# Two graph-attention layers: the second pair's projection goes through DRAM, residual loads are spread, the opening gets four row buffers

## The chip, the cores and the metric

The kernel runs on one core of one Trainium2 chip. A core has five engines, each with its own queue that it works off in order: TensorE (PE in the profile; its weight loads are a row of their own, PEld), VectorE (DVE), ScalarE (ACT), GpSimd (POOL) and SyncE (SP), which here only starts DMAs. Engines wait for one another by semaphores. DMAs are started by SP, ACT and POOL.

The metric is device time in microseconds (us). Before the change the median of three runs was 2545.72 us (2536.66 to 2552.91). The profile comes from one more execution, which took 2237.41 us.

## The reference

Two graph-attention layers run on N = 4096 nodes with a dense 0/1 adjacency matrix of int32 that holds about 32 neighbours per row (each entry is set with a chance of 1/256, the matrix is made symmetric). Cut to what matters:

```
def gat0(x, adj):                       # 8 heads of 128
    Wh  = einsum('nf,hfd->hnd', x, W)
    e   = leaky_relu(Wh@a1 [:,:,None] + Wh@a2 [:,None,:], 0.2)
    att = softmax(where(adj > 0, e, -9e15))
    hp  = elu(att @ Wh)                 # heads side by side, 1024 wide
    return hp @ W_out + b_out
x = layernorm(x + gat0(x, adj))
def gat1(x, adj):                       # 4 heads of 64
    xt  = einsum('ni,hio->hno', x, W)
    e   = leaky_relu(src + dst, 0.2)
    att = softmax(where(adj > 0, e, -inf))
    return att @ xt                     # heads side by side, 256 wide
x = layernorm(x + gat1(x, adj))
```

## The kernel before, in words

**Layer 1 (gat0) is sparse.** The factors exp of the scores let the attention be a product and a maximum, without an exponential per edge. A table in DRAM holds for each node its 256 features of x, a one, the two score factors of each head, and words of adjacency bits. There are two copies of the table, used by the phases in turn. The rows are handled in 32 tiles of 128 and in 8 phases of four tiles. A tile takes 8 steps of 16 target rows, so the loop has NG = 256 steps n (from L1209 on). For a step, GpSimd starts four indirect DMAs (L882), each of which gathers 128 rows of the table by a list of ids into a row buffer G (pool "rows", six buffers; gathers run AHEAD = 5 steps before their use). Every fourth step there is one shared gather more (Gs, L897). VectorE weighs the gathered rows (L987 to L1002), TensorE adds them up in PSUM (po, L1010), ScalarE divides (ag, L1034), TensorE and ScalarE transpose (pa L1041, aT L1044). Per tile, `close0` does the heads' projection (ph L1070), elu, the output projection (py L1093), the residual, the normalisation, stores the row tile in x1_d (L1118) and transposes it into x1T (pz L1121, L1122). Its pieces are worked off one per step from a list named `late`. When eight tiles, a chunk, are done, the following tiles' pieces are given the scores of layer 2 for that chunk and two steps of the projection for layer 2 (`step1`, pw L858 and wh L867: 16 matmuls, then 8 activations, for four row tiles).

**The lists of ids** of phase s + 2 are made while phase s runs: `words_of` loads adjacency (aq, L572), turns it to bf16 (mb, L582 or L584) and counts it into words by TensorE (L596); `lists_of` takes the largest entries by eights on VectorE (L673), transposes (lst L733, pl L738) and writes ids (L751).

**The opening** makes the lists of phase 0 out of adjacency loaded into the row buffers (tiles Ga), and the scores of layer 1: `Scores.chunk` for each of four chunks, with factors L418 (VectorE), L422 and L425 (ScalarE) in a tile `row` with one buffer, a transpose (pr L433), a store of the row to r_d by ScalarE's queue (L443), and the factors of the table's rows (L454, L457), stored into the table's tail columns by `publish` (L703). `inputs` copies x into the table (L549). Words of phase 1 begin in the opening (L827): six pieces there, the others two per step in the loop. After the opening come the first gathers.

The whole of layer 1, with the opening, has its order on each engine written out by hand (manual schedule): an instruction stands in its engine's queue where the program text puts it.

**Layer 2 (gat1) is dense.** Two pairs of heads g, four chunks c of 1024 target columns, and 32 source tiles j. For each (g, c, j) SP loads a 128 x 1024 block of the adjacency (L1308, four buffers), ScalarE makes a mask of it (mb, L1309), VectorE makes the weights of two heads (e, L1496), and TensorE multiplies them with the projected features wh (L1327, 16 matmuls) and with the row factors for the denominators (L1339, 8 matmuls). The features of the first pair are projected in layer 1, those of the second pair in (g, c) = (0, 2) by eight steps of `prepare1` from `late`. y_sb holds the residual rows, loaded from x1_d by four DMAs of 1 MB each (L1470). `unit1` divides and adds after each chunk; the last units also normalise (L1424 to L1439), in the end with four scalings in a row on ScalarE (L1436), each followed by a store. Layer 2's order on each engine is set by a scheduler, not by hand.

The last lines of the program run a general path if a flag is set; with this input it isn't.

Of the kernel before, what the change touches and what calls it, by code (L numbers as in the profile page):

```python
# [262 lines left out]
def fast_path(  # L263
# [72 lines left out]
    class Scores:  # L336
# [29 lines left out]
        def chunk(self, k, src):  # L366
# [41 lines left out]
            def factors():  # L408
                if k == 0:
# [5 lines left out]
                row = held["row"] = small.tile(  # L415
                    [P, HC], F32, tag="row", name=f"row_{n}_{k}", bufs=1
                )
# [71 lines left out]
    zero = const.tile([1, RW], F32, name="zero")  # L489
    nc.gpsimd.memset(zero, 0.0)  # L490
# [55 lines left out]
    def inputs(i, k):  # L546
        if k == 0:
            nc.sync.dma_start(table[i][N : N + 1, :], zero)
        nc.sync.dma_start(table[i][ts(k, CH), 0:F], x[ts(k, CH), :])  # L549

    lists = [None] * NPH
    words = {}

    def words_of(s):
# [7 lines left out]
        def load(m):  # L562

            k, t, q = m // (PT * PQ), m // PQ % PT, m % PQ
            if s == 0:
                G = gpool.tile([P, NB, RW], F32, tag="G", name=f"Ga_{m}")
# [20 lines left out]
        def count(m):  # L587
# [17 lines left out]
            if t == PT - 1 and q == PQ - 1:  # L605
# [9 lines left out]
                )  # L615

# [174 lines left out]
    def opening():  # L791
# [51 lines left out]
    def prepare1(g, pool):  # L843

        cj = sc1.cj
        wh = pool.tile([P, NT, 2, D1], F32, tag="wh", name=f"wh_1_{g}", bufs=1)
        w_sb = pool.tile([P, KC, 2 * D1], F32, tag="w", name=f"w_1_{g}", bufs=1)

        def first():
            nc.sync.dma_start(  # L850
                w_sb, w1f[:, ts(g, 2 * D1)].rearrange("(c p) d -> p c d", p=P)
            )

        def step(m):
            pw = ps_m.tile([P, 4, 2 * D1], F32, tag="m", name=f"pw_1_{g}_{m}")
            for jj in range(4):
                for c in range(KC):
# [3 lines left out]
                        w_sb[:, c, :],  # L861
                        start=(c == 0),
                        stop=(c == KC - 1),
                    )
            for jj in range(4):
                for k in range(2):
                    nc.scalar.activation(  # L867
                        wh[:, m + jj, k, :],
                        pw[:, jj, ts(k, D1)],
                        AF.Copy,  # L870
                        scale=cj[:, m + jj, 2 * g + k : 2 * g + k + 1],
                    )

        return wh, first, step
# [174 lines left out]
    def close0(i, aT):  # L1049
# [64 lines left out]
        def flip(k):  # L1114
# [10 lines left out]
            if turned[q] == CT:  # L1125
                fs = sc1.chunk(q, x1T[0])
                steps = [lambda m=m: step1(m) for m in range(q * CT, q * CT + CT, 4)]
# [17 lines left out]
        due = st0["due"] = st0.pop("then", {})  # L1145
        due.setdefault(0, []).append(add)
# [16 lines left out]
    now1, first1, step1 = prepare1(0, wpool)  # L1163
    late.add(load1, first1, lambda: sc1.weights(a1_sb, w1T_sb))
# [7 lines left out]
    FIRST_COUNT = 10  # L1172
# [22 lines left out]
    with tc.manual_schedule():  # L1195
# [12 lines left out]
        shared[0].weigh()  # L1208
        for n in range(NG + SOON + 1):  # L1209
            i, o, s = n // GT, n % GP, n // GP  # L1210
            busy = 0.0
            if n < NG:
# [10 lines left out]
                if o == GP - AHEAD and s + 2 < NPH:  # L1223
# [10 lines left out]
                if n % 4 == 1 and 0 < n // 4 <= NCH:  # L1234
                    inputs(1, n // 4 - 1)
# [113 lines left out]
    def unit1(g, c, po):  # L1349
# [48 lines left out]
        def norm(i0):  # L1398
# [51 lines left out]
    def verdict():  # L1450
# [17 lines left out]
    late.add(  # L1468
        *(
            lambda c=c: nc.sync.dma_start(  # L1470
                y_sb[:, ts(c, CT), :], x1_d[ts(c, CT)].rearrange("t p f -> p t f")
            )
            for c in range(NCH)
        )
    )
    for g in range(G):
        wh = now1
        for c in range(NCH):
            po = open1(g, c)
            if c == NCH - 2 and g + 1 < G:  # L1480
                now1, first1, step1 = prepare1(g + 1, rpool)
                late.add(first1, *(lambda m=m: step1(m) for m in range(0, NT, 4)))
# [3 lines left out]
            for j in range(NT):  # L1486
                if g + c == 0 and j == NT - CT:
                    late.all()
# [12 lines left out]
                if j >= 2:  # L1501
                    late.some(2 if g + c == 0 else 1)
# [81 lines left out]
```

## Time and profile before

| what | value |
|---|---|
| median of three runs | 2545.72 us (2536.66 to 2552.91) |
| profiled execution | 2237.41 us, its span 2235.6 us |
| mean granted TensorE clock, profiled | 0.957 |
| busy: PE, DVE, ACT, POOL | 89%, 87%, 39%, 48% of the span |
| DMA traffic | 443.55 MB, mean 198 GB/s |
| first gather (Gs, L897) | 85.67 us after the start |
| last gather | 1477.9 us |
| first mask weights of layer 2 (e, L1496) | 1511.5 us |
| last scaling (L1436) begins | 2227.8 us |

The span runs from the first to the last instruction of the one core. "Busy" counts instructions' own time; waiting is told apart by what ended it ("<-" and the releaser). "Issue" is idle time in which the engine waited for nothing that the profile shows. A granted clock of 1.00 is TensorE's full speed. A row of waits reads: engine, tile and line that waited, what released it, total us, times, longest us. A row with "q" behind the engine's name (SPq) is the queue of the engine's DMA issues.

### The profile page before, as it was taken

The numbers are of one execution on the slowest core, as the hardware profiler recorded it, in microseconds if no ns is written. First come the engines' busy times: TensorE is split into PE (matmuls) and PEld (weight loads), VectorE is DVE, ScalarE is ACT, GpSimd is POOL, SyncE is SP. The second block draws the span as 40 slices with busy tenths as digits, with TensorE's granted clock in tenths as the row PEclk, the third lists the DMA queues.
The fourth block names the chain that finished last, engine by engine and source line by source line (L and its number), as shares of the span: only waits on it lengthen the run. The fifth ranks groups of instructions, "written<-read, shape, count | busy, mean of one in ns | idle before, by whom it ended". The sixth has DMA issues, their size and how long they took to land.

```text
span 2235.6 us, 35623 instructions
## 1 busy us (share of the span) xinstructions
PE 1996.7 (89%) x12481; PEld 1142.5 (51%) x12481; DVE 1955.2 (87%) x4117; ACT 882.9 (39%) x1826; POOL 1077.9 (48%) x1154
## 2 busy tenths in 40 slices
PE   5487888989989999989888899888999999999996
PEld 2255566666666666666665667664424333333332
DVE  6579899999989999988999988747998899999996
ACT  1333424424334334334432233234445444465563
POOL 1377777777777777777777777730000000000000
PEclk9589999989999999999999999999999999999998
DMA  9799677578567677667665555538665566676762
GB/s 323 192 297 258 180 206 245 152 198 249 158 178 239 180 182 231 192 178 216 205 143 150 150 153 139 147 114 298 218 196 191 168 216 217 204 229 223 224 211 87
DMA packets 184149, 443.55 MB, mean 198 GB/s; under 512 B 60788, under 2 KB 92535, under 8 KB 183959
## 3 DMA queue, kind: packets, MB, share of 16 engines
q1 hardware_dynamic: 125814, 265.99, 37.9%
q0 software_dynamic: 52224, 169.97, 27.8%
q10 hardware_dynamic: 5920, 5.21, 0.8%
q8 instruction: 101, 1.65, 0.3%
q14 instruction: 90, 0.73, 0.1%
HBM read 426.04 MB, written 23.40 MB: 201 GB/s over the span
## 4 chain that ended last, share of the span: by engine, by line
PE 44%; DVE 33%; DMA 11%; issue 4%; POOL 4%; ACT 2%; SPq 1%; DVEq 0%; ACTq 0%; POOLq 0%
PE po L1327 20%; PE po L1339 10%; PE po L1010 9%; DMA G<-table,ids 7%; DVE e L988 5%; DVE e L994 5%; DVE e L1002 5%; POOL G L882 4%; DVE side L987 2%; DVE side L996 2%; PE py L1093 1%; DVE lst L673 1%; PE pw L858 1%; DVE hT L1084 1%; DVE side L916 1%
## 5 line engine op out<-in xcount | busy, mean ns | idle before, releaser
L882 POOL DMA_INDIRECT G<-table,ids x1024 | 977.9, 955 | 319.0 <-issue 234.1
L1496 DVE SCALAR_TENSOR_TENSOR e<-rb,pj,mb 128x1024 f32<-128x1024 f32 x512 | 635.5, 1282 | 58.9 <-PE po L1339 27.8
L1010 PE MATMUL po<-G,e 128*128 128x257 f32 x2048 | 553.5, 416 | 75.9 <-DVE e L1002 75.6
L1327 PE MATMUL po<-e,wh 128*32 128x512 f32 x4096 | 531.3, 595 | 7.1 <-DVE e L1496 7.1
L1010 PEld LDWEIGHTS po<-G,e 128*128 128x128 f32 x2048 | 392.1, 201 | 222.2 <-DVE e L1002 119.8
L1309 ACT ACTIVATE mb<-aq 128x1024 bf16<-128x1024 int32 x256 | 271.1, 1061 | 321.5 <-DVE e L1496 264.4
L1339 PE MATMUL po<-e,cj 128*32 128x512 f32 x2048 | 315.2, 594 | 0.0
L1411 POOL TENSOR_SCALAR nm<-nm 128x4 f32<-128x4 f32 x6 | 5.5, 911 | 640.6 <-ACT ju L1410 640.6
L1327 PEld LDWEIGHTS po<-e,wh 128*32 128x32 f32 x4096 | 149.7, 110 | 290.9 <-issue 252.6
L1034 ACT ACTIVATE ag<-po,rd_all 128x256 f32<-128x256 f32 x256 | 121.5, 475 | 321.0 <-DVE rd_all L1030 317.0
L1044 ACT COPY aT<-pa 128x256 f32<-128x256 f32 x256 | 94.8, 370 | 377.9 <-PE pa L1041 371.1
L1010 PE MATMUL po<-own,eo 128*128 128x257 f32 x512 | 166.3, 407 | 62.5 <-ACT ag L1034 57.8
L988 DVE TENSOR_TENSOR e<-rb,side 128x512 f32<-128x512 f32 x256 | 175.8, 687 | 9.1 <-DVE side L987 0.3
L994 DVE TENSOR_TENSOR e<-e,side 128x512 f32<-128x512 f32 x256 | 175.7, 686 | 8.9
L1002 DVE TENSOR_TENSOR e<-e,side 128x512 f32<-128x512 f32 x256 | 175.7, 686 | 8.8
L1010 PE MATMUL po<-Gs,e_s 32*128 32x257 f32 x512 | 182.0, 435 | 1.5 <-DVE e_s L931 1.5
L1070 PE MATMUL ph<-aT,w_sb 128*128 128x128 f32 x1024 | 145.6, 287 | 11.8 <-DVE hT L1084 11.6
L1339 PEld LDWEIGHTS po<-e,cj 128*32 128x32 f32 x2048 | 80.3, 110 | 147.3 <-issue 135.2
L1070 PEld LDWEIGHTS ph<-aT,w_sb 128*128 128x128 f32 x1024 | 135.1, 199 | 26.4 <-DVE hT L1084 12.4
L584 ACT ACTIVATE mb<-aq,half 128x1024 bf16<-128x1024 int32 x112 | 128.6, 1151 | 36.4 <-issue 18.6
L1093 PE MATMUL py<-wo_sb,hT 128*128 128x256 f32 x512 | 125.4, 388 | 0.0
L1010 PEld LDWEIGHTS po<-Gs,e_s 32*128 32x128 f32 x512 | 76.0, 185 | 89.3 <-issue 87.1
(171 smaller groups left out, 1907.3 us busy)
## 6 DMA issues: line engine op xcount, KB each, us to landing
aq<-in_adjT SPq DMA_DIRECT2D x256, 512.0 KB
aq<-in_adj SPq DMA_DIRECT2D x112, 512.0 KB
rb<-r_d SPq DMA_DIRECT2D x48, 512.0 KB
G<-table,ids POOLq DMA_INDIRECT x1024, 3.4
table<-in_x SPq DMA_DIRECT2D x8, 1024.0 KB
table<-tail SPq DMA_DIRECT2D x56, 98.0 KB
own<-table SPq DMA_DIRECT2D x32, 152.5 KB
Ga<-in_adj SPq DMA_DIRECT2D x8, 512.0 KB
```

Source lines behind the costliest of these rows:

```text
L584: nc.scalar.activation(mb, raw.pop(m), AF.Sign, bias=half[:, 0:1])
L882: nc.gpsimd.indirect_dma_start(out=G[:, b, :], out_offset=None, in_=table[s % 2][:, :], in_offset=bass.IndirectOffsetOnAxis(ap=lists[s][:, ...
L988: nc.vector.tensor_tensor(e, rb[:, :, ts(n % GT, T)].unsqueeze(1).to_broadcast(sh), f_p[:, :, 0:H0].unsqueeze(3).to_broadcast(sh), ALU.mult,)
L994: nc.vector.tensor_tensor(e, e, f_p[:, :, H0:].unsqueeze(3).to_broadcast(sh), ALU.max)
L1002: nc.vector.tensor_tensor(e, e, nb_p.unsqueeze(2).to_broadcast(sh), ALU.mult)
L1010: nc.tensor.matmul(po, w.rearrange("p h t -> p (h t)"), v[:, 0 : F + 1], start=first, **kw)
L1070: nc.tensor.matmul(phs[k][:, hh, :], w_sb[:, c, ts(h, D0)], aT[:, c, h, :], start=(c == 0), stop=(c == KC - 1),)
L1093: nc.tensor.matmul(pys[0], hT[:, h, :], wo_sb[:, h, :], start=False, stop=(h == H0 - 1))
L1309: nc.scalar.activation(mb, aq, AF.Relu, scale=OPEN)
L1327: nc.tensor.matmul(po[q][ts(b, DQ), :], wh[:, j, k, d : d + DQ], es[k][:, ts(q, HB)], start=(j == 0), stop=(j == NT - 1), tile_position=(0 ...
L1339: nc.tensor.matmul(po[NQ][r0 : r0 + DQ, :], sc1.cj[:, j, 2 * g + k : 2 * g + k + 1].to_broadcast([P, DQ]), es[k][:, ts(q, HB)], start=(j = ...
L1496: nc.vector.scalar_tensor_tensor(e, rb[k], sc1.pj[:, j, h : h + 1], mb, ALU.max, ALU.min)
```

## The change

1. **Opening.** The four chunks' `row` tiles of layer 1's scores lie in the four buffers of the weights' tag "e" instead of in one buffer.
2. **Zero rows.** The zero row of both tables is written at the start, from a tile of the pool `two`. The copies of x into the second table stand at steps n = 10, 14, 18, 22 instead of 5, 9, 13, 17.
3. **Words of phase 1.** When the opening's score pieces are used up, the first seven loads (EARLY = 7) are issued together, three into the usual buffers and four into row buffers. Their seven conversions and counts come after the first gathers, just ahead of the loop; the other nine follow two per step, each issuing a further load. The words of phase 2 begin at step 13 instead of 10, and its lists are turned at step 31 instead of 27.
4. **Projection for the second pair.** `prepare1` becomes a class, `Projected`. Six of the eight steps of the second pair, those of chunks 0 to 2, are done in layer 1's loop two tiles after the first pair's; ScalarE writes them into a staging tile (wo, in the one buffer of tag "row") and SP stores them in a DRAM tensor wh1_d, 256 KB each. Layer 2 fetches these 1.5 MB into wh, and only the steps of the last chunk stay there.
5. **Residual loads.** One 1 MB load of y_sb at every eighth step j of the first unit, instead of four in a row from `late`; `late` gives one piece per step everywhere, and is not emptied at j = 24.
6. **Last scaling.** In the last unit the odd ones of the scalings are done by VectorE, the even ones by ScalarE.

The diff, cut to its core:

```diff
@@ Scores.chunk, factors
-                row = held["row"] = small.tile(
-                    [P, HC], F32, tag="row", name=f"row_{n}_{k}", bufs=1
-                )
+                if n == 0:
+                    row = two.tile([P, HC], F32, tag="e", name=f"row_{n}_{k}", bufs=4)
+                else:
+                    row = small.tile([P, HC], F32, tag="row", name=f"row_{n}_{k}", bufs=1)
+                held["row"] = row
...
@@ inputs
-        if k == 0:
-            nc.sync.dma_start(table[i][N : N + 1, :], zero)
+        if i + k == 0:
+            for t in table:
+                nc.sync.dma_start(t[N : N + 1, :], zero[0:1, :])
...
@@ words_of
-            if s == 0:
-                G = gpool.tile([P, NB, RW], F32, tag="G", name=f"Ga_{m}")
+            if s == 0 or (s == 1 and 3 <= m < EARLY):
+                G = gpool.tile([P, NB, RW], F32, tag="G", name=f"Ga_{s}_{m}")
...
+        if s == 1:
+            def then(m):
+                convert(m)
+                count(m)
+                k = m + EARLY if m < 3 else m + 3 if m >= EARLY else NW
+                if k < NW:
+                    load(k)
+            for m in range(EARLY):
+                load(m)
+            return [lambda m=m: then(m) for m in range(NW)]
...
@@ opening
-        firsts.add(*words_of(1))
...
-            if m in (24, 26, 31, 33, 35, 37):
-                firsts.some()
+            if not scored.items and not firsts.items:
+                firsts.add(*words_of(1))
...
@@ prepare1 -> class Projected, step(m, away=False)
+            if away:
+                o = small.tile([P, 4 * 2 * D1], F32, tag="row", name=f"wo_1_{g}_{m}", bufs=1)
             for jj in range(4):
                 for k in range(2):
+                    a = 2 * jj + k
                     nc.scalar.activation(
-                        wh[:, m + jj, k, :],
+                        o[:, ts(a, D1)] if away else self.wh[:, m + jj, k, :],
...
+            if away:
+                nc.sync.dma_start(wh1_d[m // 4], o)
+        def fetch(self, m):
+            nc.sync.dma_start(
+                self.wh[:, 0:m].rearrange("p (m a) k d -> p m (a k d)", a=4),
+                wh1_d[0 : m // 4].rearrange("m p w -> p m w"),
+            )
...
@@ close0
+                if q < NCH - 1:
+                    st0["later"] = {
+                        2 + k: [lambda m=m0 + 4 * k: pair[1].step(m, True)] for k in range(2)
+                    }
...
+        if "later" in st0 and due:
+            st0["then"] = st0.pop("later")
...
@@ the loop of layer 1
-    FIRST_COUNT = 10
+    FIRST_COUNT = 13
...
+        firsts.some(EARLY)
         for n in range(NG + SOON + 1):
...
-                if o == GP - AHEAD and s + 2 < NPH:
+                if o == (GP - AHEAD if s else GP - 1) and s + 2 < NPH:
...
-                if n % 4 == 1 and 0 < n // 4 <= NCH:
-                    inputs(1, n // 4 - 1)
+                if n % 4 == 2 and 2 <= n // 4 < 2 + NCH:
+                    inputs(1, n // 4 - 2)
...
@@ scale
-                nc.scalar.activation(
-                    ys[k], ys[k], AF.Identity, bias=b[:, k : k + 1], scale=v[:, k : k + 1]
-                )
+                bk, vk = b[:, k : k + 1], v[:, k : k + 1]
+                if end and k % 2:
+                    nc.vector.tensor_scalar(ys[k], ys[k], vk, bk, ALU.mult, ALU.add)
+                else:
+                    nc.scalar.activation(ys[k], ys[k], AF.Identity, bias=bk, scale=vk)
...
@@ layer 2
-                now1, first1, step1 = prepare1(g + 1, rpool)
-                late.add(first1, *(lambda m=m: step1(m) for m in range(0, NT, 4)))
+                nxt1, m1 = pair[g + 1], NT - CT
+                nxt1.into(rpool)
+                nxt1.fetch(m1)
+                late.add(*(lambda m=m: nxt1.step(m) for m in range(m1, NT, 4)))
...
-                if g + c == 0 and j == NT - CT:
-                    late.all()
+                if g + c == 0 and j % CT == CT - 2:
+                    k = ts(j // CT, CT)
+                    nc.sync.dma_start(y_sb[:, k, :], x1_d[k].rearrange("t p f -> p t f"))
...
-                    late.some(2 if g + c == 0 else 1)
+                    late.some()
```

More of the change, by code (lines that the diff above doesn't have):

```diff
@@ L488, in fast_path @@
     nc.gpsimd.memset(tail[:, :, 0:1], 1.0)
-    zero = const.tile([1, RW], F32, name="zero")
-    nc.gpsimd.memset(zero, 0.0)
+    zero = two.tile([P, RW], F32, tag="own", name="zero")
+    nc.gpsimd.memset(zero[0:1, :], 0.0)
     bit = const.tile([P, T], I32, name="bit")
@@ L546, in inputs @@
     def inputs(i, k):
-        if k == 0:
-            nc.sync.dma_start(table[i][N : N + 1, :], zero)
+        if i + k == 0:
+            for t in table:
+                nc.sync.dma_start(t[N : N + 1, :], zero[0:1, :])
         nc.sync.dma_start(table[i][ts(k, CH), 0:F], x[ts(k, CH), :])
+    EARLY = 7
     lists = [None] * NPH
@@ L841, in fast_path, with __init__, into, first @@
     )
[L843 to L849, printed above, removed]
+    wh1_d = dram.tile([NT // 4, P, 4 * 2 * D1], F32, name="wh1_d")
+    class Projected:
+        def __init__(self, g, pool):
+            self.g = g
+            self.w = pool.tile([P, KC, 2 * D1], F32, tag=f"w{g}", name=f"w_1_{g}", bufs=1)
+        def into(self, pool):
+            self.wh = pool.tile([P, NT, 2, D1], F32, tag="wh", name=f"wh_1_{self.g}", bufs=1)
+        def first(self):
+            g = self.g
             nc.sync.dma_start(
-                w_sb, w1f[:, ts(g, 2 * D1)].rearrange("(c p) d -> p c d", p=P)
+                self.w, w1f[:, ts(g, 2 * D1)].rearrange("(c p) d -> p c d", p=P)
             )
-        def step(m):
+        def step(self, m, away=False):
+            g = self.g
             pw = ps_m.tile([P, 4, 2 * D1], F32, tag="m", name=f"pw_1_{g}_{m}")
@@ L860, in step @@
                         x1T[0][:, c, ts(m + jj, P)],
-                        w_sb[:, c, :],
+                        self.w[:, c, :],
                         start=(c == 0),
@@ L864, in step @@
                     )
+            if away:
+                o = small.tile([P, 4 * 2 * D1], F32, tag="row", name=f"wo_1_{g}_{m}", bufs=1)
             for jj in range(4):
                 for k in range(2):
+                    a = 2 * jj + k
                     nc.scalar.activation(
-                        wh[:, m + jj, k, :],
+                        o[:, ts(a, D1)] if away else self.wh[:, m + jj, k, :],
                         pw[:, jj, ts(k, D1)],
                         AF.Copy,
-                        scale=cj[:, m + jj, 2 * g + k : 2 * g + k + 1],
+                        scale=sc1.cj[:, m + jj, 2 * g + k : 2 * g + k + 1],
                     )
-        return wh, first, step
+            if away:
[5 more added lines that the diff above has]
+            )
     def gather(n):
@@ L1126, in flip @@
                 fs = sc1.chunk(q, x1T[0])
-                steps = [lambda m=m: step1(m) for m in range(q * CT, q * CT + CT, 4)]
+                m0 = q * CT
+                steps = [lambda m=m: pair[0].step(m) for m in (m0, m0 + 4)]
                 st0.setdefault("due", {}).setdefault(7, []).append(fs[0])
                 st0["then"] = {k + 1: [f] for k, f in enumerate(fs[1:] + steps)}
+                if q < NCH - 1:
+                    st0["later"] = {
+                        2 + k: [lambda m=m0 + 4 * k: pair[1].step(m, True)] for k in range(2)
+                    }
         due = st0.pop("due", {})
@@ L1161, in load1 @@
         nc.sync.dma_start(w1T_sb[0], w1T.rearrange("h d f -> d h f"))
-    now1, first1, step1 = prepare1(0, wpool)
-    late.add(load1, first1, lambda: sc1.weights(a1_sb, w1T_sb))
+    pair = [Projected(g, wpool) for g in range(H1 // 2)]
+    pair[0].into(wpool)
+    late.add(load1, pair[0].first, pair[1].first, lambda: sc1.weights(a1_sb, w1T_sb))
     NG = NT * GT
@@ L1467, in fast_path @@
     rb = targets1(0, 0)
[L1468 to L1475, printed above, removed]
     for g in range(G):
-        wh = now1
+        wh = pair[g].wh
         for c in range(NCH):
```

## The prediction

> **What bounds the kernel now.** I first set the profiled execution (2237.41 us, span 2235.6) against the runs (median 2545.72): the runs are 308 us longer, so I need to know which engine would stretch. The page's first two parts show two halves, one with GpSimd active and one without:
>
> ```profile
> PE 1996.7 (89%) x12481; PEld 1142.5 (51%) x12481; DVE 1955.2 (87%) x4117; ACT 882.9 (39%) x1826; POOL 1077.9 (48%) x1154
> ...
> POOL 1377777777777777777777777730000000000000
> PEclk9589999989999999999999999999999999999998
> DMA  9799677578567677667665555538665566676762
> ```
>
> The table by stages, whose columns are window, length, and busy time of PE, weight loads, DVE, ACT and POOL, then granted clock, DMA share and GB/s, splits it: a stretch of layer 1, the start of layer 2, a plain stretch of layer 2, and the projection of the second pair.
>
> ```profile
> 500.00:700.00 200.00, 183.01 (x862) 126.73 (x861) 182.87 (x504) 78.78 (x183) 151.53 (x158) 0.95 0.71 203
> ...
> 1530.00:1540.00 10.00, 10.00 (x66) 4.36 (x70) 8.87 (x8) 5.64 (x6) 0.00 (x0) 0.70 0.88 293
> 1540.00:1711.00 171.00, 171.00 (x1571) 68.19 (x1567) 161.75 (x139) 77.00 (x103) 0.00 (x0) 1.00 0.67 219
> 1711.00:1750.00 39.00, 39.00 (x340) 20.76 (x336) 21.19 (x18) 22.45 (x73) 0.00 (x0) 1.00 0.42 130
> ```
>
> Layer 2 is TensorE without a gap. Layer 1 looks balanced (183 of 200), so I read what its gathers waited for: the group and GpSimd's row of waits.
>
> ```profile
> L882 POOL DMA_INDIRECT G<-table,ids x1024 | 977.9, 955 | 319.0 <-issue 234.1
> ...
> POOL G L882 <- issue: 234.1, 772, 0.3
> POOL Gs L897 <- DMA aq<-in_adj: 77.5, 1, 77.5
> POOL G L882 <- PE po L1010: 22.5, 71, 0.8
> ```
>
> A gather is 0.955 us plus 0.30 us of issue gap, 1.25 us; 1,088 of them are 1,363 of the 1,392 us between the first (85.7) and the last (1477.9). In this execution GpSimd's issue bounds layer 1, and PE, 17 us in 200 behind it, hides its own additions.
>
> In the runs I infer otherwise. PE needs 183.01 x 0.95 x (5.44/200) = 4.73 us a step at full clock (256 steps, 5.44 us each). Layer 2 is 725 us at full clock. With 137 us of opening and hand-over, a clock c gives 137 + (725 + 256 x 4.73)/c; 2545.72 asks for c = 0.80. Then a step's PE work is 5.9 us, over GpSimd's 5.4: **in the runs layer 1 is probably bound by TensorE.** This is an inference from two times, and decides one part below.
>
> Last, the waits of the opening (45 to 100 us) and of the hand-over (1500 to 1540), and their pieces of the chain:
>
> ```profile
> DVE row L418 <- DMA r_d<-row: 12.1, 3, 5.4
> PE pl L738 <- ACT lst L733: 4.7, 1, 4.7
> DVE ids L751 <- PE pl L740: 4.6, 1, 4.6
> ACT mb L584 <- DMA aq<-in_adj: 4.4, 1, 4.4
> ...
> ACT mb L1309 <- DMA aq<-in_adjT: 17.3, 9, 13.4
> DVE e L1496 <- ACT mb L1309: 7.2, 1, 7.2
> PE po L1327 <- DVE e L1496: 7.1, 2, 5.2
> ```
> ```profile
> 63.83 6.64 DMA r_d<-row
> 78.73 6.93 DMA aq<-in_adj
> ...
> 1509.48 4.80 SPq L1470
> 1517.36 10.06 DMA aq<-in_adjT
> ```
>
> The first says that the scores stand three times on a store out of the single row buffer, and that the last list (lst, pl, ids) then stands on ACT behind a conversion of phase 1 (mb) whose load is late. The second: SyncE spends 1506.5 to 1517.2 issuing four 1 MB residual loads, and the mask load behind them lands 10 us later.
>
> **What the skill says.** The Trainium skill, "DMA: Bandwidth & Descriptors", section "Issuing engines are not separate DMA queues": DMAs of SyncE, ScalarE and GpSimd run on the same 16 engines and interleave. The trace agrees: the DMA share is 0.75 to 0.97 while the 4 MB and the mask loads go together, 1525 to 1540. "TensorE: Matmul & The Clock Gate", "Part 1: The HAM clock gate": an idle array falls to half clock and needs about 3.4 us of work. Here 5.2 us of idle were followed by a granted 0.50 for about 5.5 us. The same part, under "Seeing it yourself", states a limiter at 13/16 (0.81) when three cores of a die work densely. My c is close to it, but one core runs here, the trace has 0.95 to 1.00, and whether neighbours were busy isn't visible; I use c, not the rule.
>
> **The change, part by part** (profiled execution, then runs).
>
> *Four row buffers in the opening.* The three waits, 4.3, 2.4 and 5.4 = 12.1 us, go. Next late: the second chunk's ACT step still waits for the tables' x rows, landed at 59.4, as tail_0 did before; the last chunk's tail (issued at 75.0) now waits instead for its loads below and for the tail before it.
>
> *Seven words' loads at once, conversions after the list.* lst, pl and ids no longer stand behind the 4.4 us conversion: ids at 85.1 less 4.6 gives about 80, and less where the scores finish earlier. Added: four more 512 KB loads early, 2 MB, at 230 to 300 GB/s 7 to 9 us of all engines, put into the near-empty stretch 70 to 76 us and what lies before it. The changed program's last tail waits for one of them. So the first gather comes at 75 to 81 against 85.7. The four loads occupy row buffers of gathers 2 to 5; these are issued at 88 or later, the conversions, 1.15 us each, are done by then. Cost nothing, under that cover; without it, some 3 us. **Gain A: 3 to 10, taken 7.** The zero rows (one more DMA of 1 KB), the shifted table loads (n = 10 to 22 in place of 5 to 17), the count of phase 2 (13 in place of 10) and the later turn (n = 31) fill no slot that is late: the lists have until n = 27 of the next phase. Cost 0; bounds -3 to +3, as a 1 MB load is 4 us of DMA at 250 GB/s.
>
> *Residual loads spread.* SP now has one 1 MB load (2.7 us of issue) per eight steps, in place of 10.8 us together. PE idled 5.2 us (to 1529.9) and then ran some 5 us at half clock, 2.5 us of work lost: 7.7. Each later load has 4 mask buffers, 10 us, of cover, so I expect no new stall. **Gain B 7.7;** in the runs steps are longer (2.575/0.8 = 3.2 us, four buffers 2.5 us more cover), so 4.
>
> *Six of the eight projection steps into layer 1.* A plain layer-2 step is 2.575 us (1.72 + 0.86 for the two L1327/L1339 parts); in 1711 to 1750 one with a projection is 4.70. So 2.12 us x 6 = 12.7 leave layer 2 (at c = 0.8: 15.9). Into layer 1 go six times 16 matmuls (1.8 us of PE), 8 activations (0.33 us median in the pair that is there already, hidden: ACT is 39% busy) and a 256 KB store; later a 1.5 MB fetch (6 us of DMA at 250 GB/s), issued in layer 2's first chunk, three chunks ahead of its use. Profiled: PE has 17/200 x 5.44 = 0.46 us of slack a step and five gathers of lead, which hides it: **gain C 12.7.** In the runs, PE-bound: 1.8/0.8 x 6 = 13.5 us come back, and 0 to 0.5 us each for the PSUM buffer (a next tile's flip behind the activations): **net C -0.6 to +2.4, taken +1.**
>
> *Last scaling.* The chain's end has four scalings of 0.52 us in a row; two of them go to DVE, beside ACT: at most 1.0 less. **Gain D 0.8.**
>
> Sum, profiled: 7 + 7.7 + 12.7 + 0.8 = 28 of 2237, 1.25%: 2209. In the runs: 7 + 4 + 1 + 0.8 = 13, so 2545.72 - 13 = **2533**.
>
> **Rivals.** *Layer 1 stays GpSimd-bound in the runs.* Everything of C is kept: 7 + 5 + 15.9 + 0.8 = 29 to 33: 2513 to 2517, and the upper end with A = 10 at 2508. For it: the profile is so. Against: nothing else in it explains 308 us. *The opening doesn't gain* because the 2 MB sit in front of the last tail and of own_0's load in SP's queue: A = 0, 2537 to 2541. For it: tail_0 took 10 us under load against 1.6 to 3.3 alone; against: 70 to 76 us is empty. *The change doesn't unbind the hand-over:* SP's first mask loads may be held by DVE, not by issue; then B = 0, within the range. *Slower: ACT stands on the one staging buffer (wo).* The activations of m = 4, 12, 20 write into the buffer that the step before, one step (5.4 us) earlier, is still storing. That store is in SP's queue behind row loads of the next tile; SP's wait for DVE there was 591 us over 30 times, longest 41.9. It decides from 5.4 us of hold plus about 2 for landing; a hold of 20 to 40 us puts ACT, behind which ag, aT and masks wait, into three stalls of 12 to 34 us net of two steps' cover: 35 to 100 us less 13 of gain, 2568 to 2633. Against: the step is placed five steps after the tile's row loads, by when they had been released.
>
> **Chances.** Likeliest (PE-bound layer 1) 0.50, 2521 to 2543, with about 0.08 of it past 25 us of gain; GpSimd-bound 0.27; opening without gain 0.11; slower 0.12, of which 0.09 beyond 1%. A difference of 1%, 25 us, is about what a measurement can tell, as runs of one kernel span 16. Faster by over 1% (under 2520): 0.27 + 0.08 = 0.35; slower (over 2571): 0.09; the rest 0.56. Leaving out about one in ten at each side, the range is 2506 to 2552.
>
> **What would show it.** Opening: no DVE wait of row on r_d in phase 0, first gather (Gs) at 75 to 81. Hand-over: no PE idle over 1 us near 1500, clock 1.00 by 1530. Layer 2: two projection steps of 4.7 us, not eight; span of the period with GpSimd active unchanged within 5 us in a profile at 0.95. If that period grows by 10 us or more in the profile, C's cover is not there. ACT waiting for wh1_d's store over 5 us would show the slower rival. The prediction is wrong if the runs follow the profile's 1.25% (GpSimd-bound), or if the early loads push tail_3 past 80.

## The result, and the profile after

The changed kernel took 2530.68 us (median of 22 runs, 2513.07 to 2550.55) against 2544.72 us before (22 runs, 2530.75 to 2570.59): a ratio of 0.9942, 95% interval 0.9923 to 0.9961, that is 14 us or 0.6% less. The forecast was 2533 us. The changed kernel's profiled execution took 2532.02 us, span 2530.2. All ratios here and below are worked out from the single runs and not as the quotient of the medians given beside them, and they leave out runs over 1.5% above the fastest of their kernel, of which there is one, of six, in the third set of runs of the changed kernel.

One thing must be known to read all that follows: chips differ, and on the chip of the first profile, and on that of the first four experiments (chip A below), the kernel before takes 2236 to 2237 us, while on those of the result above and of the other experiments (B and C) it takes 2540 to 2548. So the first profile of before is not one of the runs that the forecast is measured by; that of after is. The page of after, its first two parts:

```profile
PE 2133.9 (84%) x12481; PEld 1217.2 (48%) x12481; DVE 1967.2 (78%) x4121; ACT 872.1 (34%) x1822; POOL 1083.4 (43%) x1154
...
POOL 1455566566655666666566666656100000000000
PEclk9578888889878899888888889988999999999998
DMA  9777657456535746655564644444396666666763
```

The table by stages of after (columns as in the prediction), layer 1 and layer 2:

```profile
100.00:1780.00 1680.00, 1360.78 (x5759) 940.59 (x5758) 1229.57 (x3304) 487.35 (x1189) 1039.80 (x1086) 0.86 0.56 157
1840.00:2500.00 660.00, 660.00 (x6074) 213.93 (x6070) 626.23 (x527) 330.18 (x517) 16.26 (x24) 1.00 0.67 220
```

All of the difference between the chips lies in layer 1 (the table of all profiles below: 1386 against some 1700 us, with layer 2 the same). Layer 2 is at full clock here too, so there is no clock that is low everywhere. In layer 1 the mean clock is 0.86, and no engine is busy throughout. What GpSimd and VectorE wait for, one row of before and then after:

```profile
DVE rd_all L1029 <- PE po L1010: 26.3, 13, 4.5
```
```profile
POOL G L917 <- issue: 256.2, 824, 1.2
...
POOL G L917 <- DVE rd_all L1064: 156.7, 59, 9.7
DVE rd_all L1064 <- PE po L1045: 153.0, 72, 11.0
...
POOL G L917 <- PE po L1045: 82.3, 48, 4.7
```

GpSimd, which before waited for products in crumbs of 0.3 us (at most 0.8), now stands up to 9.7 us; rd_all (VectorE's reading of the sums) and the next gathers are released together, by a finished product (po). GpSimd's issue costs about what it did (256 us against 234); what is new on this chip is the waiting for TensorE's products (156.7 and 82.3 us for GpSimd).

The opening of after (waits from 40 to 100 us) and its hand-over (1828 to 1860):

```profile
POOL Gs L932 <- DVE eo L1010: 71.9, 1, 71.9
...
ACT row L424 <- DMA aq<-in_adj: 5.1, 1, 5.1
```
```profile
ACT mb L1353 <- DMA aq<-in_adjT: 4.2, 3, 3.2
DVE e L1537 <- DMA r_d<-row: 3.2, 1, 3.2
PEld po L1371 <- DVE e L1537: 2.4, 8, 0.6
```

No wait of the rows of scores for r_d is left in VectorE (12.1 us before), nor one of pl on lst over 0.3 us. The second line is new: ScalarE's part of the last row of scores now waits for one of the early loads, which the prediction had said of the last tail. At the hand-over the mask's longest wait is 3.2 us (13.4 before), and TensorE's products have no gap over 1 us until the first chunk ends.

In the table of all profiles below, layer 1 runs from the start of the first product of rows gathered into G (po<-G, L1010 of before) to the end of the last, layer 2 from the first product of masked weights (L1327) to the end of the last; "tail" is the rest of the span. A single layer 1 varies: the changed kernel's three are 1699 to 1711 us, those of the first profile and of chip A with layer 1 as before 1385.6 to 1386.9. So does the first gather: three kernels of chip A whose opening makes the same lists in the same order have it at 86.2, 84.8 and 83.3 us.

| kernel | chip | first gather | layer 1 | layer 2 | tail |
|---|---|---|---|---|---|
| before, first profile | | 85.7 | 1385.6 | 702.5 | 20.3 |
| before again | A | 86.2 | 1386.9 | 700.0 | 20.5 |
| projection alone | A | 84.8 | 1393.1 | 687.2 | 20.0 |
| opening alone | A | 80.9 | 1382.8 | 700.9 | 20.2 |
| residual loads alone | A | 83.3 | 1386.7 | 693.3 | 20.4 |
| after, result | | 80.1 | 1707.4 | 681.0 | 20.6 |
| after again | B | 78.7 | 1699.3 | 681.0 | 21.0 |
| without the projection | B | 78.1 | 1681.0 | 694.4 | 20.3 |
| activations a step later | B | 77.9 | 1685.6 | 680.8 | 20.6 |
| transposes done twice | B | 78.6 | 1685.6 | 681.1 | 20.7 |
| after, a third time | C | 83.1 | 1710.8 | 680.6 | 20.8 |
| activations a step later | C | 83.3 | 1705.6 | 681.8 | 20.6 |
| row buffers alone | C | 81.3 | 1698.2 | 699.6 | 20.5 |
| moved matmuls three times | C | 83.1 | 1737.2 | 680.6 | 20.7 |

### The profile page after: what moved, and what is told of

It is laid out like the page before. It is cut to its first block, busy times and chain, and to the rows that moved or that the text cites. A ratio compares the mean times of both kernels' runs of the same rounds, so it can differ in the third digit from the quotient of the medians.

```text
span 2530.2 us, 35637 instructions
## 1 busy us (share of the span) xinstructions
PE 2133.9 (84%) x12481; PEld 1217.2 (48%) x12481; DVE 1967.2 (78%) x4121; ACT 872.1 (34%) x1822; POOL 1083.4 (43%) x1154
## 4 chain that ended last, share of the span: by engine, by line
PE 66%; another core or an unknown queue 13%; DVE 8%; ACT 7%; issue 4%; DMA 2%; POOL 0%; ACTq 0%; DVEq 0%; POOLq 0%; SPq 0%
PE po L1045 27%; PE po L1371 18%; PE po L1383 9%; PE py L1128 3%; PE ph L1105 3%; PE pa L1076 2%; ACT ag L1069 1%; ACT mb L588 1%; ACT rb_s L944 1%; PE pw L600 1%; DVE e L1023 1%; DVE e L1029 1%; PE pw L883 1%; DMA Ga<-in_adj 1%
## 5 line engine op out<-in xcount | busy, mean ns | idle before, releaser
L1537 DVE SCALAR_TENSOR_TENSOR e<-rb,pj,mb 128x1024 f32<-128x1024 f32 x512 | 635.2, 1282 | 37.4 <-PE po L1383 13.3
L1045 PE MATMUL po<-G,e 128*128 128x257 f32 x2048 | 623.4, 456 | 17.8 <-DVE e L1037 7.7
L1045 PEld LDWEIGHTS po<-G,e 128*128 128x128 f32 x2048 | 435.6, 224 | 186.3 <-issue 60.2
L1045 PE MATMUL po<-own,eo 128*128 128x257 f32 x512 | 188.9, 454 | 237.6 <-ACT ag L1069 181.6
L1383 PE MATMUL po<-e,cj 128*32 128x512 f32 x2048 | 333.3, 592 | 0.0
L1064 DVE TENSOR_SCALAR rd_all<-po 128x1 f32<-128x1 f32 x256 | 38.7, 151 | 229.5 <-PE po L1045 153.0
L1045 PEld LDWEIGHTS po<-own,eo 128*128 128x128 f32 x512 | 86.9, 213 | 268.8 <-ACT ag L1069 202.4
L1045 PE MATMUL po<-Gs,e_s 32*128 32x257 f32 x512 | 202.7, 479 | 5.6 <-issue 5.6
L1105 PE MATMUL ph<-aT,w_sb 128*128 128x128 f32 x1024 | 152.4, 294 | 13.8 <-DVE hT L1119 6.7
L1045 PEld LDWEIGHTS po<-Gs,e_s 32*128 32x128 f32 x512 | 84.7, 206 | 105.5 <-issue 105.4
```

Source lines behind the costliest of these rows:

```text
L1045: nc.tensor.matmul(po, w.rearrange("p h t -> p (h t)"), v[:, 0 : F + 1], start=first, **kw)
L1105: nc.tensor.matmul(phs[k][:, hh, :], w_sb[:, c, ts(h, D0)], aT[:, c, h, :], start=(c == 0), stop=(c == KC - 1),)
L1383: nc.tensor.matmul(po[NQ][r0 : r0 + DQ, :], sc1.cj[:, j, 2 * g + k : 2 * g + k + 1].to_broadcast([P, DQ]), es[k][:, ts(q, HB)], start=(j = ...
L1537: nc.vector.scalar_tensor_tensor(e, rb[k], sc1.pj[:, j, h : h + 1], mb, ALU.max, ALU.min)
```

## The experiments

### The kernel before, once more

The kernel is unchanged.

> The kernel before, unchanged, for a second profile of it, since its first profiled execution took 2237 us and the runs 2545. If TensorE limits layer 1 in the runs (theory P), this execution shows layer 1 (first to last product of gathered rows) near 1,690 to 1,710 us against 1,386 in the first profile, with GpSimd waiting for buffers and some 450 us or more of half clock in it; layer 2 from its first product to its last near 702 us, as in the first. If a uniformly lower clock is the cause, as the prediction took it, layer 2 takes about 702/0.8 = 870 us and its granted clock is about 0.8.

It took 2237.92 us, with layer 1 at 1386.9 and layer 2 at 700.0 us: the first profile again, almost to the microsecond. On chip A it couldn't decide what the runs of the result do; it showed that chips differ and that 2237 us was no chance. The profile of after answers the second half of the question: layer 2 isn't at 0.8 of the clock.

### One part at a time, chip A

The projection by DRAM alone (the hunks of `Projected`, `close0`, `fetch`, put into the kernel before):

```diff
-    now1, first1, step1 = prepare1(0, wpool)
+    pair = [Projected(g, wpool) for g in range(H1 // 2)]
...
+                    st0["later"] = {
+                        2 + k: [lambda m=m0 + 4 * k: pair[1].step(m, True)] for k in range(2)
+                    }
```

> The kernel before with the projection by DRAM alone (and the zero row's tile moved, which makes room for it). Layer 2 shorter by 12.7 us in the profile. Theory P, TensorE limits layer 1: 13 us come back there, total within 6 us of before (ratio 0.998 to 1.002). Theory G, the moved steps are hidden under GpSimd's issue: the whole 12.7 stays, ratio 0.995.

Ratio 0.9975 (0.9967 to 0.9984), 2230.12 against 2235.58 us. Layer 2 became 12.8 us shorter (700.0 to 687.2), but layer 1 6.2 us longer: neither theory. Half of the gain stays. Step by step (n by the products, as their sums are read) the delay against the kernel before grows by 2.2 us at the first two moved steps (n = 101 to 104), 1.1 at the next two (165 to 168), and 10.7 at the last two (229 to 232), of which 3.7 remain at the end of the layer. The timeline of this kernel at the fifth of the six:

```profile
1361.17 1.95 PE L868 MATMUL pw<-w,x1T_sb 128*128 128x128 f32 x16
...
1363.15 1.75 ACT L880 ACTIVATE wo<-pw,cj 128x64 f32<-128x64 f32 x8 [4.41 <-PE pw L868]
...
1364.74 0.65 ACT L1100 ACTIVATE el<-ph 128x512 f32<-128x512 f32 x1
...
1365.42 0.63 ACT L1101 ACTIVATE el<-el 128x512 f32<-128x512 f32 x1
...
1365.96 0.46 ACT L1054 ACTIVATE ag<-po,rd_all 128x256 f32<-128x256 f32 x1
...
1366.47 0.94 PE L1030 MATMUL po<-own,eo 128*128 128x257 f32 x2 [2.24 <-ACT ag L1054]
...
1367.34 1.22 PE L1030 MATMUL po<-Gs,e_s 32*128 32x257 f32 x2
...
1368.49 3.79 PE L1030 MATMUL po<-G,e 128*128 128x257 f32 x8
```

ScalarE stands 4.4 us on the projection's matmuls (pw), then writes eight pieces (1.75 us), then the two of el, and only then ag, for which TensorE's next product waits 2.2 us. The products that follow are slow: eight of G take 3.79 us, against 2.00 for the eight of the step before, as the granted clock fell to 0.50 right after the gap (mean 0.70 from 1366 to 1368 us, 0.50 from 1368 to 1372). So TensorE's 0.46 us of slack a step did not hide the moved step.

The opening alone:

```diff
+                if n == 0:
+                    row = two.tile([P, HC], F32, tag="e", name=f"row_{n}_{k}", bufs=4)
...
+            for m in range(EARLY):
+                load(m)
...
+        firsts.some(EARLY)
```

> The kernel before with the opening's changes alone: four row buffers, seven early loads, the order of words and table loads. First gather at 79 to 81 us against 85.7. If that gain is kept through layer 1, total 5 to 6 us shorter, ratio 0.998. If the early words' loads cost steps of the first phase (the changed kernel's profile has steps of 24.7 and 16.4 us at n = 2 and 5), ratio 1.000 to 1.008, and these long steps appear here and not in a profile of the kernel before.

Ratio 0.9974 (0.9966 to 0.9981), 5.8 us less; first gather at 80.9 us and nothing lost after it. The two long steps at the start of after's profile (25.4 and 16.4 us) don't appear here, so the early loads alone don't make them. The first belongs to the other chips: the kernel with the row buffers alone, which has no early loads, has it on chip C too (24.5 us). It doesn't have the second, and what makes that one stays open. What the first gather waits for in this kernel:

```profile
POOL Gs L913 <- DMA table<-tail: 72.7, 1, 72.7
```

It is the last tail's store, as the prediction said of what is late next.

The residual loads alone:

```diff
-                if g + c == 0 and j == NT - CT:
-                    late.all()
+                if g + c == 0 and j % CT == CT - 2:
+                    k = ts(j // CT, CT)
+                    nc.sync.dma_start(y_sb[:, k, :], x1_d[k].rearrange("t p f -> p t f"))
```

> The kernel before with the residual loads spread alone. Prediction's profiled sum: no gap of TensorE over 1 us after the first masks, layer 2 shorter by 7.7 us, total ratio 0.997 in the runs if layer 2 runs at full clock, 0.9985 (4 us) if the clock is 0.8 there. Nothing of layer 1 is touched.

Ratio 0.9971 (0.9964 to 0.9979), 6.6 us less; layer 2 shorter by 6.7 us against the same chip's profile of before (9.2 against the first one). TensorE's longest wait for VectorE at the hand-over (1504 to 1545 us) is 1.2 us, against 5.2:

```profile
PE po L1327 <- DVE e L1489: 1.2, 1, 1.2
```

On chip A the kernel before had a gap of 4.6 us there and one piece of half clock, 3.4 us, that is 1.7 us of work lost: 6.3 together, which is the gain. How long SyncE was held by the four loads, before and here (shortest, median and longest in ns):

```profile
L1470 SPq DMA_DIRECT2D y_sb<-x_d x4: 530/2653/4796, 1506.5 to 1514.3; - x4
```
```profile
L1481 SPq DMA_DIRECT2D y_sb<-x_d x4: 428/428/494, 1509.9 to 1550.2; - x4
```

One load of 1 MB held SyncE for 0.43 us where it stood alone, and for 2.4 to 4.8 us where it stood behind another of its kind. So the spreading took away most of the issuing time itself, and not only its place.

### The parts together, and one left out, chip B

The changed kernel, unchanged:

> The changed kernel, unchanged, beside the kernels of its parts on one chip. The three parts alone gave ratios of 0.9975, 0.9974 and 0.9971; if they add up, 0.992, and the profile shows first gather near 80 us, layer 2 (first to last product) near 681 us and the tail after it as before (20.3 us), so that the last scaling brings nothing.

Ratio 0.9908 (0.9875 to 0.9941), 2520.88 against 2539.72 us. The three gains of chip A add up to 17.9 us (5.5, 5.8 and 6.6), which of 2544.72 us is a ratio of 0.993; that lies in this interval, in that of the result and in that of the third time. The tail is 20.3 to 21.0 us in all kernels with the last scaling on two engines and 20.0 to 20.5 in those without: it brought nothing.

Without the projection:

```diff
-                    st0["later"] = {
-                        2 + k: [lambda m=m0 + 4 * k: pair[1].step(m, True)] for k in range(2)
-                    }
...
-                nxt1.fetch(m1)
-                late.add(*(lambda m=m: nxt1.step(m) for m in range(m1, NT, 4)))
+                late.add(first1, *(lambda m=m: step1(m) for m in range(0, NT, 4)))
```

> The changed kernel with the second pair's projection back in layer 2, all else kept. The projection alone gave 0.9975, half of the 12.7 us that layer 2 lost in its profile. Theory P (the moved steps are paid for in layer 1, through TensorE and through what stands behind the 8 activations on ScalarE): layer 2 is 13 us longer than in the changed kernel, layer 1 6 to 13 us shorter; ratio 0.9945 to 0.996 where the changed kernel has 0.992 or 0.994. Theory G (hidden): layer 1 the same, ratio 0.998.

Ratio 0.9968 (0.9944 to 0.9993), 2531.66 us. Layer 2 is 13.4 us longer than in after again, layer 1 18 us shorter. By the two profiles the projection brings nothing here, rather a loss; by the runs it brings 0.006 (some 0.002 to 0.010, from the two half-widths 0.0033 and 0.0025 taken together). The profiled execution of this kernel (2517.59 us) was the second fastest of its 20 runs, 14 us under their median, so the runs count more. Their interval (0.9944 to 0.9993) holds the ratios of both theories: how much of the 13.4 us comes back isn't settled on this chip. On chip A it is half.

### Is it ScalarE's standing?

The eight activations and the store of a moved step are issued in the next step of the loop, behind ag and aT:

```diff
             if away:
-                o = small.tile([P, 4 * 2 * D1], F32, tag="row", name=f"wo_1_{g}_{m}", bufs=1)
+                drains.append(lambda: self.drain(m, pw, True))
...
                 flip(n - SOON - 1, ag, done)
+            while drains:
+                drains.pop(0)()
```

> The changed kernel, with the 8 activations and the store of each moved step issued in the next loop step, behind ag and aT on ScalarE, so that ScalarE doesn't stand on the projection's matmuls with the next ag behind it. If that wait (4 to 8 us of ScalarE at a moved step in the profile of the projection alone) is what layer 1 pays, layer 1 is 4 to 7 us shorter than in the changed kernel, ratio 0.002 to 0.003 below it. If TensorE's 1.8 us a step is what it pays, the same time within 3 us.

> The changed kernel with the activations of each moved step one loop step later, again, to narrow its interval. If ScalarE's standing on the projection is what the moved steps cost in layer 1, 0.002 to 0.003 below the changed kernel beside it; if their 1.8 us of TensorE are, within 0.001 of it.

On chip B 0.986 (0.981 to 0.991) beside 0.9908; on chip C 0.9906 (0.9871 to 0.9942) beside the changed kernel's 0.9892 (0.9841 to 0.9942). ScalarE no longer waits for a moved step at all (16.4, 9.0 and 8.2, together 33.6 us in six waits in after again on chip B; 0 here), and layer 1 was 13.7 and 5.2 us shorter in the profiles, but the ratios differ by -0.005 and +0.001, each by less than its uncertainty of about 0.006. Inconclusive: the wait is gone, a gain isn't shown.

The changed kernel beside it on chip C:

> The changed kernel again, beside the three below. If the parts' gains add (0.9975, 0.9974 and 0.9971 alone), ratio 0.990 to 0.994; layer 2 from its first product to its last 681 us; first gather 78 to 81 us.

Ratio 0.9892 (0.9841 to 0.9942), from five runs; 2532.33 us, the median of all six, against 2548.27. First gather at 83.1 us: later than on the other chips, and outside what was expected.

### More work for TensorE, in two places

Each step's two transposes done twice:

```diff
-        for c in range(KC):
+        for c in 2 * list(range(KC)):
             nc.tensor.transpose(
```

> The changed kernel with the two transposes of each layer-1 step (pa) done twice, the second over the first: 256 x 0.55 us = 141 us more work for TensorE at full clock, and nothing else. If GpSimd bounds layer 1 with 0.46 us of TensorE's slack a step, it grows by 0.1 to 0.2 us a step, 25 to 50 us. If TensorE bounds it, by the whole 141 us or more. If the half clock after idle stretches is what bounds it, the extra work keeps the clock up (half clock in layer 1 well under that of the changed kernel) and layer 1 grows by much less, or shrinks.

Ratio 0.989 (0.9842 to 0.9938) beside 0.9908. The work added was less than was expected of it, since these instructions overlap: the group of transposes is busy 162.6 us instead of 105.4, 57 more. Layer 1 didn't grow: 1685.6 us against 1699.3. The stage of layer 1 in both, after again first:

```profile
100.00:1770.00 1670.00, 1343.95 (x5752) 931.81 (x5751) 1226.45 (x3302) 485.09 (x1186) 1034.29 (x1085) 0.86 0.55 158
```
```profile
100.00:1755.00 1655.00, 1378.43 (x6247) 972.49 (x6246) 1227.39 (x3302) 486.32 (x1186) 1036.94 (x1085) 0.88 0.56 159
```

The mean clock is 0.88 instead of 0.86. As the clock's record has the states 1.00 and 0.50 alone, that is (1 - 0.88) x 2 x 1655 = 397 us of half clock instead of (1 - 0.86) x 2 x 1670 = 468. This is the third of the outcomes expected: work spread evenly over layer 1 cost nothing here. Whether that is because the sum of TensorE's work doesn't bound layer 1, or because the added work was paid for by the clock that it kept up (71 us less of half clock, an estimated 35 us of work), this run can't tell.

The moved steps' matmuls done three times over:

```diff
-            for jj in range(4):
+            for jj in (3 if away else 1) * list(range(4)):
                 for c in range(KC):
```

> The changed kernel with the 16 matmuls of each of the six moved steps done three times over: 6 x 3.6 us = 22 us more work for TensorE in layer 1, and ScalarE waits 3.6 us longer at each. If layer 1 has room for it (GpSimd's pace, 0.46 us a step and the gathers' lead), under 6 us more than the changed kernel, ratio up by at most 0.0025. If a moved step is paid in full by whoever stands behind it, 20 to 30 us more, ratio up by 0.009 to 0.013.

Ratio 1.0067 (1.0043 to 1.0091), 2565.97 us beside 2532.33 us; layer 1 1737.2 against 1710.8. So 22 us of work in six places cost 26 us in the profile, 34 by the medians and 45 by the ratios (0.0175, give or take 0.006): paid in full and more. What ScalarE waited for at the moved steps in this kernel:

```profile
ACT wo L895 <- PE pa L1076: 47.8, 4, 13.4
...
ACT wo L895 <- remote: 19.3, 2, 10.0
```

67 us in six waits, against 31.5 in the changed kernel on the same chip (20.4, 7.0 and 4.1). The releaser named is the transposes that stand next after the moved step's products. Concentrated work was paid for here, where evenly spread work, on chip B, cost nothing. That the six steps cost as they do because of ScalarE's waits, with ag behind it, is the likeliest reading, not a shown one: the runs that took the waits away didn't confirm it beyond their uncertainty, and the 22 us are also work in TensorE's own queue.

### Which part of the opening

The four row buffers alone:

```diff
+                if n == 0:
+                    row = two.tile([P, HC], F32, tag="e", name=f"row_{n}_{k}", bufs=4)
+                else:
+                    row = small.tile([P, HC], F32, tag="row", name=f"row_{n}_{k}", bufs=1)
```

> The kernel before with the four row buffers of the opening alone. The three waits of the scores for r_d (9 to 12 us together) are gone. Prediction's order of things: the last list stands behind the conversion of a word of phase 1, whose load lands at 83 us, so the first gather stays at 84 to 86 us and the time the same (ratio 0.999 to 1.001). If the row buffers alone bring it forward, it comes at 79 to 81 as with the whole opening, ratio 0.9975.

Ratio 0.9975 (0.9956 to 0.9993); first gather at 81.3 us, on a chip where the whole opening gives 83.1 to 83.3. (The kernel before has no profile on this chip; on chip A it has 86.2.) The expectation of no gain failed: the buffers alone bring one as large as the whole opening's on chip A. Its waits of 45 to 100 us:

```profile
POOL Gs L899 <- DMA aq<-in_adj: 73.1, 1, 73.1
...
PEld pl L740 <- ACT lst L735: 6.4, 1, 6.4
DVE ids L753 <- PE pl L742: 6.4, 1, 6.4
...
ACT mb L586 <- DMA aq<-in_adj: 6.0, 1, 6.0
```

The list still stands behind the conversion, and longer (6.4 against 4.6 us), but all of it is earlier, which fits the program's order: the words' loads alternate with the scores' pieces, and these no longer wait.

That the first gather is no earlier with the whole opening doesn't mean that the early loads and the new order did nothing. The ids of the last list, in the row buffers alone and in the third after, both on chip C:

```profile
80.67 0.30 DVE L753 TENSOR_SCALAR ids<-pl 128x136 int32<-128x136 f32 x1 [6.36 <-PE pl L742]
```
```profile
75.80 0.30 DVE L769 TENSOR_SCALAR ids<-pl 128x136 int32<-128x136 f32 x1
```

The list is 4.9 us earlier with the whole opening (in the four profiles with neither part it is written by 83.0 to 85.8 us), and it no longer decides. The last packet of the last tail, of 196 bytes, ends at 74.3 us in the row buffers alone, and at 80.4 in the third after, where that store is issued 4.0 us later and goes beside the early loads; the first gather follows at 83.1. In the eight other profiles with the whole opening it is the same: the list is written by 73.8 to 78.0 us, and the first gather starts 2.0 to 3.5 us after the last packet of the last tail. In two of the nine the profile names the tail's store as what released it; in the others this is read from the times. So each half of the opening does what it was made for, and on chip C the second half's gain is taken back by the tail that it delays.

## Why the prediction was right, and where its steps were not

**The total.** 2533 us forecast, 2530.68 measured; 13 us less forecast, 14 measured, with an interval of some 10 to 20. The total and the range hold, but that the forecast lies so near is in part luck. The terms for the runs were 7, 4, 1 and 0.8 us; one at a time on chip A they were 5.8, 6.6, 5.5 and nothing. The two that were too small were made so by a step that failed, the clock of 0.8. The sum of the measured terms is 17.9 us, which the result's interval doesn't tell from 13.

**What bounds the kernel.** For the first profile, GpSimd's issue in layer 1 is right: layer 1 stays within about 1 us when nothing of it is touched, and the opening's earlier start comes out at the end. For the runs the step "137 + (725 + 256 x 4.73)/c ... c = 0.80" failed. There is no clock of 0.8: layer 2 has 1.00, and as it stood before it takes 700.0 us on chip A and 699.6 on chip C, and layer 1 has stretches of half clock and waits. (The 137 us also count some of layer 2 twice: 2235.6 less 725 and less 256 x 5.44 leaves 118. The c stays at 0.80 with it.) Nor is layer 1 bound by the amount of TensorE's work as that step has it: in after TensorE is idle for 319 of the 1680 us of that stage. It was right that more than GpSimd's issue holds layer 1 in the runs. Whether the projection's gain was paid back there, which the forecast drew from it, isn't settled on chip B; about half of it was paid back on chip A, where GpSimd does bound layer 1.

**Opening, gain A, 3 to 10, taken 7.** 5.8 us of time on chip A: right in size. First gather 5.3 us earlier than in before again, but 2.4 than in the residual loads alone, whose opening is that of before; one execution has that much play. Right in its division too: the row buffers bring the scores forward, the early loads and the order of the conversions the list ("about 80, and less", measured 77.0). Right in what is late next, the last tail, but not in its size: the forecast's own sign of failure, "if the early loads push tail_3 past 80", came true, or came within 0.2 us of it, in the three profiles of chip C with the early loads (last packet at 79.8, 80.3 and 80.4 us), and there the row buffers alone do as well. The rival "the opening doesn't gain" named this mechanism in part, the 2 MB in front of the last tail.

**Residual loads, gain B, 7.7.** Measured 6.6, from the gap and the half clock after it as the forecast had it. "2.7 us of issue" for each spread load was wrong: 0.43 us. The step that cut the gain to 4 for the runs was wrong, as it rested on the clock of 0.8: layer 2 on chip C is 19.0 us shorter in after than with the row buffers alone (699.6 to 680.6), which is B and the projection's 12.8 together, 6.2 for B.

**Projection, gain C.** 2.12 us a step, 12.7 in layer 2: measured 12.8 and 13.4. In the profiled regime the step "0.46 us of slack a step and five gathers of lead, which hides it" failed: 6.2 us come back. What it left out was who stands behind: in the timeline above ScalarE waits for the matmuls at the head of its queue, with ag behind it. For ScalarE the prediction counted its busy share, 39%, and took it as hidden. (That the 6.2 us go when this wait goes isn't shown.) In the runs, "net C -0.6 to +2.4, taken +1" was too low: after and its version without the projection differ by 0.006, 15 us, somewhere from 5 to 25 (11 by the medians), and on chip A 5.5 us stay.

**Last scaling, gain D 0.8.** Nothing. The scalings of the first half now sit on VectorE ahead of the statistics of the second, as the end of after's timeline shows, VectorE alone:

```profile
2518.07 0.70 DVE L1482 TENSOR_SCALAR y_sb<-y_sb,nm,nm 128x256 f32<-128x256 f32 x2
2518.70 0.75 DVE L1471 BATCH_NORM_STATS2 st<-y_sb 128x6 f32<-128x256 f32 x2
...
2521.28 0.73 DVE L1482 TENSOR_SCALAR y_sb<-y_sb,nm,nm 128x256 f32<-128x256 f32 x2
```

The second half's scalings start 11.7 us after the last product instead of 11.0, which takes back most of what the shorter last row saves (1.09 us instead of 2.07); the eight stores of SyncE then end the span. The prediction priced the moved instruction on the engine that it left and not on the one that it went to.

**Rivals.** The slower one, ScalarE waiting for the store out of the one staging buffer, didn't happen: in no profile is a DMA what wo waits for; where a releaser is named, it is TensorE. The GpSimd-bound one, 29 to 33 us less, lies outside the result's interval (its lower end with A = 10 comes to 2510 by its own terms, not 2508).

**DMAs of different engines.** The loads that the prediction offers as sharing the 16 DMA engines, 1525 to 1540 us, are all SyncE's. Layer 1 shows what it meant: from 500 to 520 us of before, GpSimd's gathers took 39.6% and SyncE's transfers 43.1% of the engines' time.

**The sum for the runs.** About 5 us of opening, 19 to 21 of layer 2, less what layer 1 gives back, some 6 on chip A and 13 or so by the profiles of chip C (1698.2 to 1710.8), make 11 to 20; 14 was measured. A single layer 1 has some 12 us of play, so this is no more than agreement in size.

## What to carry to other kernels

Work that is moved under another bound is not hidden because its engine has slack: ask what stands in order behind each of its instructions on every engine that it touches, above all behind the one that drains its result. When one of two late things is made earlier, ask what its new transfers do to the other: the list came 5 us earlier, and the tail 6 us later. Before a profile's regime is carried over to runs that take 14% longer, look for the stage in which the time lies; a uniform factor was the wrong guess. And when a step goes to a second engine, price it in that engine's queue too.

## What the runs showed of the hardware

The kernel before takes 2236 us on chip A and 2540 to 2548 us on others, all of the difference in one stage. Between chips A and B the median durations of the costliest instructions agree within 3 ns (DVE weights of layer 2 1282 and 1281, gathers 949 and 949, products of gathered rows 380 and 380). Two things differ. One is the clock: in layer 1 (1370 us of before again, 1650 of after) TensorE worked at half clock for 122 and 383 us. Half of that is lost work, so the clock makes up an estimated 130 us of the 320, and it may follow from the waits instead of causing them. The other is when products count as done. In before again, all 13 times that rd_all waited for a product it started 0.04 us after the recorded end of that product. In after, of the 96 waits over 0.3 us a quarter started more than 5.1 us after it, the longest 19.5. That longest one, in after's timeline, VectorE, ScalarE and GpSimd:

```profile
124.04 0.16 DVE L1064 TENSOR_SCALAR rd_all<-po 128x1 f32<-128x1 f32 x1 [20.09 <-remote]
124.13 2.19 ACT L588 ACTIVATE mb<-aq,half 128x1024 bf16<-128x1024 int32 x2 [22.48 <-remote]
...
124.27 0.95 POOL L917 DMA_INDIRECT G<-table,ids  x1 [5.31 <-remote]
```

Three engines are released within 0.3 us; the product that rd_all needs has its recorded end at 104.5 us. Such delays of over 5 us recur at the same steps in the nine profiles of these chips (n = 1 in all nine, n = 28 in eight, n = 12 and 173 in six each), so they hang on the program's place and not on chance alone. Their cause stays open: the profile's ends of matmuls are modelled, and none of the runs told a late start of the matmuls from a late signal of their end.

The halving of the clock comes in pieces of 3.4 us, as the Trainium skill describes it ("TensorE: Matmul & The Clock Gate", "Part 1: The HAM clock gate"), and doesn't need a gap as long as that: in the first profile of before, TensorE was busy for 0.56 by the median, at most 0.77, of the 29 full-clock pieces with any work that a halved one followed, and in 26 of them no single gap was longer than 2.6 us. The busy share alone doesn't decide: pieces with as little as 0.49 were followed by full clock.

SyncE was held for 0.43 us by a 1 MB load that stood alone, and for 2.4 to 4.8 us by one right behind another; what holds it there, the runs don't show.
